# Attention without a maxima pass: exponentials taken unshifted, their sums tested, the old program kept behind a branch

## The chip, the cores and the metric

The kernel runs on one core of a Trainium2 chip. The core has five engines that matter here: TensorE (PE in the profile; its weight loads are the row PEld), VectorE (DVE), ScalarE (ACT), GpSimd (POOL) and SyncE (SP), which only issues transfers. Matmuls read SBUF and write PSUM, which has eight banks of 512 fp32 numbers on each of 128 partitions. The metric is the device time of one execution in microseconds; lower is better. The whole program is unrolled: there is no loop on the chip, so every instruction in the profile is one that was written out.

## The reference

```python
# x: [4, 512, 48, 48]; t = 48*48 = 2304 tokens, 8 heads of d = 64
hn = group_norm(x, 32 groups) * gn_scale + gn_bias
qkv = einsum('oc,bchw->bohw', qkv_w, hn) + qkv_b          # fp32, then to fp16
q, k, v = qkv.reshape(b, 3, 8, 64, t).astype(float16)
s = 64 ** -0.25                                            # as fp16
w = softmax(einsum('bhct,bhcs->bhts', q * s, k * s), axis=-1)
a = einsum('bhts,bhcs->bhct', w, v).astype(float32)
out = x + einsum('oc,bchw->bohw', proj_w, a) + proj_b
```

For each of 4 images and 8 heads there is a 2304 x 2304 matrix of scores, whose exponentials are summed along a row and multiplied by v.

## The kernel before

Channels lie on partitions: 512 channels are four chunks of 128, and chunk p of q, k and v is the head pair p. So there are 16 head pairs in all (4 images, 4 pairs), and tokens are cut into 6 blocks of 384 (TB) or 18 tiles of 128.

*Group norm* (`norm_items`, lines 138 to 176) takes statistics of x with VectorE, averages them over a group's channels with two small matmuls, and gets a factor and an offset per channel. The norm is applied later, by GpSimd, as each block of 384 tokens is needed (`load_hn`, line 185), once for k and once for q and v of every head pair.

*q, k, v of a head pair* (`pair_items`, line 179). For each block and each of q, k, v four fp32 matmuls (one for each channel chunk, line 203) accumulate in one PSUM bank; ScalarE moves the result out as fp16 (line 225). v then goes through three transposes (line 242) so that tokens lie on partitions.

*The maxima.* Softmax needs the largest score of each row before the exponentials. `max_tile` (line 250) computes the scores with the rows (queries) on partitions, 64 channels deep, and VectorE reduces each 128 x 384 tile to its maximum (line 263). `put_max` (line 265) turns minus the maximum into two fp16 numbers and moves them with small matmuls into two extra rows beside q. The product of k, with ones in those rows, and q is then the score minus its maximum.

*Attention* (`attend`, line 343). A step is one block of queries, one head, and two tiles of keys: two matmuls give scores with keys on partitions (line 358; 66 rows deep for the even head, 128 with zeros for the odd), ScalarE takes the exponential of 768 columns at once (line 366), and two steps later two matmuls multiply by v (line 373). v has a column of ones, so row 64 of the product is the sum of the exponentials. After a head's 18 key tiles, VectorE and ScalarE move the product and the sum out; every second block VectorE inverts four rows of sums, GpSimd spreads them over partitions and multiplies (lines 387 to 398).

*Projection* (`proj_items`, line 310): GpSimd widens the attention output to fp32, sixteen fp32 matmuls for each block (line 322), VectorE adds the bias and x (line 331), and SP's queue stores the result.

*The order.* While a pair is attended, the next pair's q, k, v and maxima, the previous image's projection and the next image's norm stand in a list of items with weights (0.64 for an fp32 matmul, 0.35 for two maxima). After each step as many items follow as keep their done weight in proportion to the steps. A scheduler then turns this into one queue for each engine; it keeps dependences and may move an instruction that is ready ahead of one that was written before it. Each engine works through its own queue in order.

PSUM: two double banks for scores, one for the product with v, two for maxima, one (`ps_w`) that q, k, v, transposes, moved maxima and projection share.

## Time and profile before

| what | value |
|---|---|
| runs | 4481.62, 4498.35, 4500.76 us; median 4498.35 |
| span of the profiled execution, first to last instruction | 4493.3 us |
| mean granted TensorE clock | 0.805 |
| PE busy, weight loads | 91%, 36% |
| DVE, ACT, POOL busy | 50%, 40%, 17% |

The profiled execution has no device time of its own beside its span; the median of the runs is 5 us above the span and the lowest 12 us below it. A matmul's end is modelled in the profile (a stream of them is pipelined, and the shown durations overlap), so spacing from start to start, or the chain of waits, tells what one costs. The granted clock is the share of full speed that the chip allowed TensorE; 0.50 is half speed.

### The profile page before, as it was taken

The page shows a single profiled execution, that of the slowest core. Times are in us where ns is not written, and L with a number is a line of the kernel's source. Part 1 is how long each engine was busy: PE and PEld are TensorE (multiplying, and loading weights), DVE is VectorE, ACT ScalarE, POOL GpSimd, SP SyncE. Part 2 cuts the span into 40 slices and gives each one's busy share as a digit, 9 for nine tenths or more (in the row PEclk, how much of TensorE's full clock was granted, in tenths as well). Part 3 has the DMA queues.
Part 4 walks back from the last instruction along what each step waited for, and adds up shares of the span by engine and source line. Part 5 has one row for each costly group of instructions (what it writes and reads, how often), then busy time and mean ns, then how long its engine had stood idle before and what let it go on. Part 6 is the DMA issues. An engine that isn't in the chain of part 4 may idle for free.

```text
span 4493.3 us, 39314 instructions
## 1 busy us (share of the span) xinstructions
PE 4079.8 (91%) x14320; PEld 1600.4 (36%) x14320; DVE 2251.2 (50%) x4323; ACT 1805.2 (40%) x2593; POOL 767.3 (17%) x1176
## 2 busy tenths in 40 slices
PE   5789999989999999999999999999999999999998
PEld 2233333333333433333333334333333444333344
DVE  5555455463545455465454555545355444554531
ACT  1144443435443343443434433354433433334462
POOL 3021211112121121211202112121211212112001
PEclk8687877878788987777878988787777988778789
DMA  3000000000000010000000001000000000000001
GB/s 122 0 1 1 1 1 0 1 1 1 1 1 16 20 50 0 1 1 1 1 1 8 15 15 50 0 1 1 1 1 0 8 20 16 0 1 1 1 2 41
DMA packets 21314, 44.48 MB, mean 10 GB/s; under 512 B 2688, under 2 KB 14976, under 8 KB 21120
## 3 DMA queue, kind: packets, MB, share of 16 engines
q1 hardware_dynamic: 18432, 37.76, 2.3%
q10 hardware_dynamic: 2688, 4.21, 0.3%
q8 instruction: 113, 1.85, 0.2%
q14 instruction: 81, 0.66, 0.1%
HBM read 23.08 MB, written 18.87 MB: 9 GB/s over the span
## 4 chain that ended last, share of the span: by engine, by line
PE 76%; DVE 16%; issue 3%; ACT 2%; POOL 1%; DMA 1%; POOLq 0%; SPq 0%; ACTq 0%; DVEq 0%
PE av L373 18%; PE pm L256 17%; PE ps L358 15%; DVE mx L263 13%; PE q L203 7%; PE v L203 6%; PE pr L322 6%; PE k L203 5%; PE mt L276 2%; DVE avs L387 1%; ACT p L366 1%; PE vtr L242 1%; DVE inv L392 1%; ACT sums L388 1%; POOL att L398 0%
## 5 line engine op out<-in xcount | busy, mean ns | idle before, releaser
L263 DVE TENSOR_REDUCE mx<-pm 128x1 f32<-128x384 f32 x3456 | 1844.9, 555 | 1386.1 <-PE pm L256 1271.0
L366 ACT ACTIVATE p<-ps 128x768 f16<-128x768 f32 x1728 | 1358.8, 808 | 939.1 <-PE ps L358 806.7
L373 PE MATMUL av<-p,vv 128*65 128x384 f16 x3456 | 1111.0, 398 | 18.0 <-ACT sums L388 17.9
L256 PE MATMUL pm<-ke,qe 64*128 64x384 f16 x1728 | 679.1, 393 | 109.3 <-DVE mx L263 82.5
L256 PE MATMUL pm<-ko,qo 64*128 64x384 f16 x1728 | 684.4, 396 | 66.2 <-DVE mx L263 22.4
L358 PE MATMUL ps<-qe,ke 66*128 66x384 f16 x1728 | 530.9, 362 | 7.6 <-ACT p L366 7.6
L373 PEld LDWEIGHTS <-vv 128*65 128x65 f16 x3456 | 390.5, 127 | 402.6 <-issue 278.5
L358 PE MATMUL ps<-qo,ko 128*128 128x384 f16 x1728 | 526.5, 358 | 1.6 <-ACT p L366 1.5
L388 ACT COPY sums<-av 1x384 f32<-1x384 f32 x192 | 90.3, 470 | 922.1 <-DVE avs L387 919.8
L256 PEld LDWEIGHTS <-qo 64*128 64x128 f16 x1728 | 165.9, 96 | 674.0 <-issue 673.3
L256 PEld LDWEIGHTS <-qe 64*128 64x128 f16 x1728 | 165.3, 96 | 638.6 <-issue 601.2
L387 DVE COPY avs<-av 64x384 f32<-64x384 f32 x192 | 105.0, 547 | 437.0 <-PE av L373 423.1
L322 PE MATMUL pr<-a,wproj 128*128 128x384 f32 x768 | 277.8, 504 | 19.5 <-DVE x L331 17.5
L358 PEld LDWEIGHTS <-ke 66*128 66x128 f16 x1728 | 167.7, 106 | 186.1 <-issue 135.6
L396 POOL PARTITION_BROADCAST ib<-inv x96 | 59.5, 677 | 955.9 <-DVE inv L392 754.4
L331 DVE SCALAR_TENSOR_TENSOR x<-pr,bproj,x 128x384 f32<-128x384 f32 x96 | 58.8, 612 | 325.8 <-PE pr L322 325.8
L358 PEld LDWEIGHTS <-ko 128*128 128x128 f16 x1728 | 155.9, 104 | 184.6 <-issue 138.3
L276 PE MATMUL mt<-ident,hl 128*2 128x128 f16 x576 | 89.7, 290 | 115.1 <-DVE hl L272 112.3
L322 PEld LDWEIGHTS pr<-a,wproj 128*128 128x128 f32 x768 | 142.2, 194 | 127.0 <-DVE x L331 39.6
L225 ACT ACTIVATE qe<-q,bqk 64x384 f16<-64x384 f32 x96 | 55.2, 575 | 266.1 <-PE q L203 266.0
L398 POOL TENSOR_TENSOR att<-avs,ib 128x384 f16<-128x384 f32 x96 | 93.4, 985 | 363.5 <-issue 363.5
L392 DVE RECIPROCAL inv<-sums 97x384 f32<-97x384 f32 x48 | 122.5, 2551 | 44.4 <-ACT sums L388 44.4
(815 smaller groups left out, 2508.1 us busy)
## 6 DMA issues: line engine op xcount, KB each, us to landing
x<-x_dram SPq DMA_DIRECT2D x32, 576.0 KB, 6.8
out_dram<-x SPq DMA_DIRECT2D x96, 192.0 KB, 1.9
wqkv<-qkv_wT_dram ACTq DMA_DIRECT2D x3, 1024.0 KB, 15.2
wproj<-proj_wT_dram ACTq DMA_DIRECT2D x1, 1024.0 KB, 14.0
gsc<-gn_scale_dram ACTq DMA_DIRECT2D x1, 2.0 KB, 4.0
gbi<-gn_bias_dram ACTq DMA_DIRECT2D x1, 2.0 KB, 5.6
bqkv<-qkv_b_dram ACTq DMA_DIRECT2D x1, 6.0 KB, 6.6
bproj<-proj_b_dram ACTq DMA_DIRECT2D x1, 2.0 KB, 6.3
```

What stands on the lines that cost most here:

```text
L203: nc.tensor.matmul(pw[name], wqkv[:, c, o : o + P], hn[key][:, c, :], start=(c == 0), stop=(c == NC - 1),)
L256: nc.tensor.matmul(pm, q[lo : lo + D, t0 : t0 + P], k[lo : lo + D, bass.ts(s, TB)], start=True, stop=True,)
L263: nc.vector.tensor_reduce(mx[:, h, i, s : s + 1], pm, AX.X, ALU.max)
L276: nc.tensor.matmul(pt[lo : lo + 2, bass.ts(i, P)], hl[:, h, i, :], ident, start=True, stop=True,)
L322: nc.tensor.matmul(pw[o], wproj[:, c, bass.ts(o, P)], at[0][:, c, :], start=(c == 0), stop=(c == NC - 1),)
L358: nc.tensor.matmul(ps[:, i, :TB], kk[0:rows, bass.ts(2 * s + i, P)], qq[0:rows, bass.ts(j, TB)], start=True, stop=True,)
L366: nc.scalar.activation(pt[k], ps[:, :, :TB], AF.Exp)
L373: nc.tensor.matmul(av[0], vv[:, 2 * s + i, h, :], pt[k][:, i, :], start=(s == 0 and i == 0), stop=(s == NT // 2 - 1 and i == 1),)
L387: nc.vector.tensor_copy(avs[j][h * D : (h + 1) * D, :], av[0][0:D, :])
L388: nc.scalar.copy(sm[r : r + 1, :], av[0][D : D + 1, :])
L392: nc.vector.reciprocal(inv[0:97, :], sm[0:97, :])
L398: nc.gpsimd.tensor_tensor(att[:, bass.ts(jj, TB)], avs[jj], ib, ALU.mult)
```

## The change

The old program becomes `general_path` (with block sizes renamed; nothing else in it is changed). A new `fast_path` runs first, and a branch on the chip runs the old program after it, over the same output, if any sum of exponentials lies outside 256 to 60000. In `fast_path`:

- there is no maxima pass: the exponential is taken of the score itself;
- a unit of attention is one block of 512 queries (the last has 256), both heads and one tile of keys (two in the last block): the two heads' scores are matmuls 64 rows deep on the upper and lower rows, and one exponential takes 1024 columns;
- the sums go by transfer to one number per partition, are inverted there, and come back through DRAM spread over 64 partitions; they are kept for the test;
- the norm is applied once, in place, by VectorE; x is loaded again for the sum at the end;
- v is computed with tokens on partitions (the normalised x is the stationary operand), so it isn't transposed;
- the projection's weights are split into a rounded part and the rest, both float32r, and each fp32 matmul becomes two of float32r;
- q, k and v are moved out of PSUM by VectorE; `ps_w` has two banks, and the product with v has one for each head;
- units go in bursts of two: two units' scores, then the values of the burst before, then items.

```diff
+SUM_MIN, SUM_MAX = 256.0, 60000.0
...
+    ps_s = ctx.enter_context(tc.tile_pool(name="ps_s", bufs=2, space=PSUM))
+    ps_av = ctx.enter_context(tc.tile_pool(name="ps_av", bufs=1, space=PSUM))
+    ps_w = ctx.enter_context(tc.tile_pool(name="ps_w", bufs=2, space=PSUM))
...
+    def split_wproj():
+        for c in range(NC):
+            w = work.tile([P, C], F32, tag="res", bufs=3, name=f"wproj_{c}")
+            nc.sync.dma_start(w, proj_wT[bass.ts(c, P), :])
+            nc.vector.tensor_copy(whi[:, c, :], w)
+            nc.vector.tensor_tensor(
+                wlo[:, c, :], w, whi[:, c, :].bitcast(F32), ALU.subtract
+            )
...
+    def norm(b):
...
+        for c in range(NC):
+            nc.vector.tensor_scalar(
+                hn[b][c],
+                hn[b][c],
+                ga[:, c : c + 1],
+                gb[:, c : c + 1],
+                ALU.mult,
+                ALU.add,
+            )
...
+    def qk_items(g):
...
+        def one(part, j, c, pw):
+            o, n = QBLOCKS[j]
+            if c == 0:
+                pw[0] = ps_w.tile([P, QB], F32, tag="pw", name=f"pqk_{g}_{part}_{j}")
+            w0 = part * C + pr * P
+            nc.tensor.matmul(
+                pw[0][:, :n],
+                wqkv[:, c, w0 : w0 + P],
+                hn[b][c][:, o : o + n],
+                start=(c == 0),
+                stop=(c == NC - 1),
+            )
+            if c == NC - 1:
+                col = part * NPAIR + pr
+                nc.vector.tensor_scalar(
+                    qk[g][part][:, o : o + n],
+                    pw[0][:, :n],
+                    SCALE,
+                    bqk[:, col : col + 1],
+                    ALU.mult,
+                    ALU.add,
+                )
...
+    def v_items(b):
...
+        def one(i, c, pw):
...
+            nc.tensor.matmul(
+                pw[0],
+                hn[b][c][:, bass.ts(i, P)],
+                wqkv[:, c, 2 * C :],
+                start=(c == 0),
+                stop=(c == NC - 1),
+            )
+            if c == NC - 1:
+                for pr in range(NPAIR):
+                    cols = bass.ts(pr, P)
+                    nc.vector.tensor_tensor(
+                        vv[b * NPAIR + pr][:, i, :, 0:D],
+                        pw[0][:, cols].rearrange("p (h d) -> p h d", d=D),
+                        bv[:, cols].rearrange("p (h d) -> p h d", d=D),
+                        ALU.add,
+                    )
...
+    def proj_items(b, j):
...
+            if c == 0:
+                pw[0] = ps_w.tile([P, QB], F32, tag="pw", name=f"pr_{b}_{j}_{m}")
+                pw[1] = work.tile([P, QB], F32, tag="res", bufs=3, name=f"x_{b}_{j}_{m}")
+                nc.sync.dma_start(pw[1][:, :n], x[b, bass.ts(m, P), o : o + n])
+            for i, w in enumerate((whi, wlo)):
+                nc.tensor.matmul(
+                    pw[0][:, :n],
+                    w[:, c, bass.ts(m, P)],
+                    at[0][:, c, :n],
+                    start=(c == 0 and i == 0),
+                    stop=(c == NC - 1 and i == 1),
+                )
...
+    def scores(u):
...
+        for a, i in enumerate(keys):
+            for h in range(2):
+                rows = slice(h * D, (h + 1) * D)
+                nc.tensor.matmul(
+                    ps[:, h, a * n : (a + 1) * n],
+                    k[rows, bass.ts(i, P)],
+                    q[rows, o : o + n],
+                    start=True,
+                    stop=True,
+                )
+        pt = ppool.tile([P, 2, QB], F16, tag="p", name=f"p_{g}_{j}_{keys[0]}")
+        nc.scalar.activation(pt, ps, AF.Exp)
...
+    def values(u):
...
+        for h in range(2):
+            for a, i in enumerate(keys):
+                nc.tensor.matmul(
+                    av[h][:, :n],
+                    vv[g][:, i, h, :],
+                    pt[:, h, a * n : (a + 1) * n],
+                    start=(i == 0),
+                    stop=(i == NT - 1),
+                )
...
+    def finish(g, j):
...
+        for h in range(2):
+            nc.vector.tensor_copy(avx[0 : D + 1, h, :n], av[h][:, :n])
+        first = 2 * o // P
+        sm = sums[:, g, first : first + 2 * per].rearrange("p (h i) -> p h i", h=2)
+        for h in range(2):
+            nc.sync.dma_start(sm[:, h, :], avx[D : D + 1, h, :n])
+        inv = small.tile([P, 2, QB // P], F32, tag="inv", name=f"inv_{g}_{j}")
+        nc.vector.reciprocal(inv[:, :, :per], sm)
+        row = dram.tile([2, QB], F32, tag="row", name=f"row_{g}_{j}")
+        nc.sync.dma_start(
+            row[:, :n].rearrange("h (p i) -> p h i", i=per), inv[:, :, :per]
+        )
+        ib = work.tile([D, 2, QB], F32, tag="ib", name=f"ib_{g}_{j}")
+        nc.sync.dma_start(
+            ib[:, :, :n], row[:, :n].unsqueeze(0).to_broadcast((D, 2, n))
+        )
+        for h in range(2):
+            nc.vector.tensor_tensor(
+                atts[g][h * D : (h + 1) * D, o : o + n],
+                avx[0:D, h, :n],
+                ib[:, h, :n],
+                ALU.mult,
+            )
...
+    beside = {g: [] for g in range(NG)}
+    for b in range(B):
+        g = b * NPAIR
+        for pr in (2, 3):
+            beside[g + pr - 2] += qk_items(g + pr)
+        if b > 0:
+            for j in range(NQ):
+                late = b == B - 1
+                beside[g + (2 + j // 3 if late else j // 4)] += proj_items(b - 1, j)
+        if b + 1 < B:
+
+            def turn(b=b):
+                hn[b + 1] = load_x(b + 1, (nc.gpsimd, nc.gpsimd))
+                norm(b + 1)
+
+            beside[g + 2].insert(0, (0.0, turn))
+            vs = v_items(b + 1)
+            beside[g + 2] += [(45.0, lambda: None)] + vs[:55]
+            beside[g + 3] += vs[55:]
+            for pr in (0, 1):
+                beside[g + 3] += qk_items(g + NPAIR + pr)
+
+    norm(0)
+    for _, run in qk_items(0):
+        run()
+    split_wproj()
+    for _, run in v_items(0) + qk_items(1):
+        run()
...
+    for n in range(0, len(stream), 2):
+        burst = stream[n : n + 2]
...
+            scores(u)
+        for u in waiting:
+            values(u)
+        waiting = burst
+        fill(n + len(burst) - 1)
...
+    nc.vector.tensor_scalar(low, flat, SUM_MIN, None, ALU.is_ge)
...
+    nc.vector.scalar_tensor_tensor(both, flat, SUM_MAX, low, ALU.is_le, ALU.mult)
...
+    nc.vector.tensor_reduce(good, both, AX.X, ALU.add)
...
+    nc.tensor.matmul(pf, good, ones, start=True, stop=True)
+    nc.vector.tensor_scalar(flag, pf, float(B * HEADS * T) - 0.5, None, ALU.is_lt)
...
+    fast_path(tc, flag, *args)
+    fails = nc.values_load(
...
+    with tc.If(fails > 0):
+        general_path(tc, *args)
```

A number beside an item is its weight; `fill` runs a pair's items in proportion to the units done, as the old list did. The weight of 45 runs nothing: it only holds back what follows it.

More of the change, by code (lines that the diff above doesn't have):

```diff
@@ L12 @@
 F32 = mybir.dt.float32
+F32R = mybir.dt.float32r
 F16 = mybir.dt.float16
+I32 = mybir.dt.int32
 AF = mybir.ActivationFunctionType
@@ L25, with general_path @@
 NPAIR = HEADS // 2
-TB = 384
-NB = T // TB
+NG = B * NPAIR
 NT = T // P
-TPB = TB // P
 SCALE = float(np.float16(1.0 / math.sqrt(math.sqrt(D))))
 LAG = 2
+GTB = 384
+GNB = T // GTB
+GTPB = GTB // P
+QB = 512
+QBLOCKS = [(o, min(QB, T - o)) for o in range(0, T, QB)]
+NQ = len(QBLOCKS)
+SB = 384
+SUM_MIN, SUM_MAX = 256.0, 60000.0
 @with_exitstack
-def group_norm_attention(
+def general_path(
     ctx: ExitStack,
@@ L347, in attend @@
         atts[g] = att
-        steps = [(j, h, s) for j in range(NB) for h in range(2) for s in range(NT // 2)]
+        steps = [(j, h, s) for j in range(GNB) for h in range(2) for s in range(NT // 2)]
         total = sum(w for w, _ in items) or 1.0
@@ L390, in values @@
                 return
-            inv = work.tile([P, TB], F32, tag="inv", name=f"inv_{g}_{j}")
+            inv = work.tile([P, GTB], F32, tag="inv", name=f"inv_{g}_{j}")
             nc.vector.reciprocal(inv[0:97, :], sm[0:97, :])
@@ L398, in values @@
                 nc.gpsimd.tensor_tensor(
-                    att[:, bass.ts(jj, TB)], avs[jj], ib, ALU.mult
+                    att[:, bass.ts(jj, GTB)], avs[jj], ib, ALU.mult
                 )
@@ L450, with group_norm_attention @@
+@with_exitstack
+def group_norm_attention(ctx: ExitStack, tc: tile.TileContext, *args):
+    nc = tc.nc
+    keep = ctx.enter_context(tc.tile_pool(name="keep", bufs=1))
+    flag = keep.tile([1, 1], I32, name="flag")
+    fast_path(tc, flag, *args)
+    fails = nc.values_load(
+        flag[0:1, 0:1],
+        min_val=0,
+        max_val=1,
+        skip_runtime_bounds_check_because="it is the result of a comparison",
+    )
+    with tc.If(fails > 0):
+        general_path(tc, *args)
 def kernel(
```

295 lines of the change are left out of this document (259 added, 36 removed).

## The prediction

> **What bounds the kernel now.** I read the busy times first, then the chain of waits, then the costliest groups.
>
> ```profile
> span 4493.3 us, 39314 instructions
> PE 4079.8 (91%) x14320; PEld 1600.4 (36%) x14320; DVE 2251.2 (50%) x4323; ACT 1805.2 (40%) x2593; POOL 767.3 (17%) x1176
> ...
> PE 76%; DVE 16%; issue 3%; ACT 2%; POOL 1%; DMA 1%; POOLq 0%; SPq 0%; ACTq 0%; DVEq 0%
> PE av L373 18%; PE pm L256 17%; PE ps L358 15%; DVE mx L263 13%; PE q L203 7%; PE v L203 6%; PE pr L322 6%; PE k L203 5%; PE mt L276 2%; DVE avs L387 1%; ACT p L366 1%; PE vtr L242 1%; DVE inv L392 1%; ACT sums L388 1%; POOL att L398 0%
> ...
> L263 DVE TENSOR_REDUCE mx<-pm 128x1 f32<-128x384 f32 x3456 | 1844.9, 555 | 1386.1 <-PE pm L256 1271.0
> L366 ACT ACTIVATE p<-ps 128x768 f16<-128x768 f32 x1728 | 1358.8, 808 | 939.1 <-PE ps L358 806.7
> ```
>
> The chain is PE three quarters of the time, and the maxima pass alone (the matmuls into pm, the reductions into mx, the move into mt) holds 17 + 13 + 2 = 32% of it, some 1440 us. ACT and DVE have slack. But the pass costs more than its 32%. The view of busy time by stretches, with the granted clock in the column after POOL, shows it:
>
> ```profile
> 200.00:4300.00 4100.00, 3780.95 (x13293) 1467.38 (x13292) 2103.86 (x4032) 1684.62 (x2417) 689.69 (x1061) 0.80 0.02 6
> 4320.00:4410.00 90.00, 86.49 (x443) 48.12 (x442) 13.04 (x17) 82.76 (x116) 13.64 (x20) 0.97 0.02 5
> 4425.00:4490.00 65.00, 51.76 (x146) 25.87 (x145) 11.17 (x19) 0.00 (x0) 7.68 (x17) 1.00 0.15 55
> ...
> 1928.00:1932.00 4.00, 2.86 (x7) 0.51 (x5) 3.94 (x8) 0.00 (x0) 0.00 (x0) 0.50 0.00 0
> ```
>
> From 200 to 4300 us, where maxima run, the clock is 0.80. In the last pair, which has attention and no maxima left, it is 0.97 while ACT is busy 82.76 of 90 us; in the closing projection it is 1.00 although PE waits a fifth of the time for evictions. The low clock sits where PE waits for DVE's maxima (the 4 us row: DVE 3.94 busy, seven matmuls, clock 0.50). So the pass goes, and the clock should come back with it.
>
> **What one matmul costs at full clock.** From the chain in order of time, and from the order on PE:
>
> ```profile
> 1502.69 2.58 PE pr L322 x8
> 1508.83 0.33 PE av L373 x2
> 1509.16 0.33 PE ps L358 x2
> ```
>
> ```profile
> 1945.96 0.33 PE L256 MATMUL pm<-ke,qe 64*128 64x384 f16 x1
> 1945.97 0.33 PE L256 MATMUL pm<-ko,qo 64*128 64x384 f16 x1
> 1946.23 0.52 PE L373 MATMUL av<-p,vv 128*65 128x384 f16 x2
> ...
> 1946.91 0.33 PE L373 MATMUL av<-p,vv 128*65 128x384 f16 x1
> 1947.16 0.33 PE L256 MATMUL pm<-ke,qe 64*128 64x384 f16 x1
> ```
>
> An fp32 matmul is two instructions (768 of pr for 384 matmuls), each 2.58/8 = 0.3225 us at 384 columns, so 0.43 at 512 and 0.215 at 256. An fp16 matmul of 384 takes 0.33/2 = 0.165, half as long as an fp32 instruction; at 512 I take half of 0.43, 0.215. The second fence holds the two prices on which the packed scores rest. Two matmuls of 64 rows, one on each half of the rows, start 0.01 apart and the next matmul starts 0.26 later: the pair runs at once. And that 0.26, like the 0.25 from av into pm, is 0.10 more than 0.165: changing between 64-row and 128-row matmuls costs 0.10 each way.
>
> **The change, part by part.**
>
> *Removed:* the 3456 matmuls and reductions of the maxima, mt and vtr, and ACT's evictions of q, k, v.
>
> *Attention.* 16 head pairs x (4 blocks x 18 + 9) = 1296 units. Each has one packed pair of scores (0.215), two products with v (0.43), and half of the two row changes of a burst of two units (0.10): 0.745 us, 966 in all. Weight loads I take as hidden, as in the chain above where each matmul has its own; if those of one pair can't load under the pair before, up to 0.10 more per unit by the row change, +130. Below 0.745 it can't go, since the row changes are in the order.
>
> *q, k:* per pair 2 x 4 channel chunks x (4 x 0.86 + 0.43) = 31.0, times 16 = 495. *v:* the same columns with tokens as the stationary side, 288 x 0.86 = 248, without transposes. *Projection:* each fp32 matmul becomes two of float32r. No row shows that type. Bounds: as costly as an fp16 pass (0.215 for 512), 4 x 16 x 2 x (4 x 0.215 + 0.108) = 124; or as an fp32 matmul each, four times that, 495. I take 124, since the instruction reads one rounded operand, which is nearest to the fp16 row. The Trainium skill ("FP8 and Floating Point Precision", TensorE Precision Notes) gives true FP32 four passes and describes a reduced FP32 read; the 0.3225 against 0.165 agrees with two passes in each of two instructions, and no run here shows the reduced form.
>
> PE's sum at full clock: 966 + 495 + 248 + 124 = 1833.
>
> *ACT* has nothing left but exponentials of 1024.
>
> ```profile
> 4359.78 4.43 ACT L366 ACTIVATE p<-ps 128x768 f16<-128x768 f32 x6
> ...
> L225 ACT ACTIVATE ke<-k,bqk 64x384 f16<-64x384 f32 x96 | 55.2, 575 | 161.3 <-PE k L203 161.0
> ```
>
> Back to back one of 768 takes 0.738. Scaled wholly it is 0.985 for 1024; with the slope between 575 and 808 ns (0.61 ns a column) 0.89. I take 0.94: 1218 in all (1153 to 1277), below PE. A unit of attention alone is 0.745 on PE against 0.94 on ACT, so wherever the fillers are missing ACT sets the pace: the first half of each third pair (a weight of 45 stands there for the loading of the next image, against 47 of v: 39 units x 0.195 = 8, three times) and the last pair (60 + 10 of PE work against 76). Together +30.
>
> *DVE* takes q, k, v evictions, the norm's application and the divisions. By the 612 ns of a 384 eviction, 160 of q and k and 80 of the projection at 0.82 are 196, 288 small ones of v about 0.35 are 100, and four of 512 for each of 80 blocks another 260: about 650 with the norm, a third of the span. It hides, unless it waits.
>
> *Waits added.* At each of the 80 block ends DVE copies, then waits for the sums to come back over SP's queue, inverts, waits for a write and a broadcast read, and multiplies. Rows for such transfers:
>
> ```profile
> out_dram<-x SPq DMA_DIRECT2D x96, 192.0 KB, 1.9
> ...
> gsc<-gn_scale_dram ACTq DMA_DIRECT2D x1, 2.0 KB, 4.0
> ```
>
> Three in series are 5.7 to 12 us. Behind the waiting reciprocal stand the evictions of q, k, v, and behind those PE, which has a second ps_w bank: one more group of four matmuls (3.4 us) and the attention among it (about 3) before it stops. So 0 to about 6 us each, 0 to 480. The order on DVE isn't the text's order, which speaks for little:
>
> ```profile
> 27.38 0.56 DVE L145 BATCH_NORM_STATS2 st<-x 128x6 f32<-128x384 f32 x1 [5.10 <-DMA x<-x_dram]
> 27.86 0.14 DVE L152 COPY mean<-gmean 128x4 f32<-128x4 f32 x1
> 27.92 0.55 DVE L145 BATCH_NORM_STATS2 st<-x 128x6 f32<-128x384 f32 x1
> ```
>
> The second image's statistics, written far behind, run between steps of the first image's norm. Work that is ready is put between waiting steps, so I take 0.75 us each, 60, with the norm's two matmuls and a late image in it. The Trainium skill ("DMA: Bandwidth & Descriptors") puts a fixed cost of about 2.0 us on every transfer. By it the chain is 6 us, at the low end, and the 60 would be nearer to nothing; the 4.0 of gsc says that small ones take longer.
>
> *Other queues.* SP takes four transfers a block (320) and, in the projection, a load of x and a store for each of 80 groups, in order: an x behind a row that waits for the reciprocal is late by the same chain, which is within the 6 us. The bytes are no matter: the closing row above has a DMA share of 0.15 at 55 GB/s. POOL has casts in place of the norm. The next image is loaded into the one set of x buffers only when its predecessor's q and k are done; the weight of 45 gives that 39 x 0.94 = 37 us, against some 40 for the load and norm at the start (next fence). Where it is late, PE has attention left to do, and each us beyond that is lost, three times.
>
> *Start.*
>
> ```profile
> 22.43 0.56 PE L150 MATMUL gmean<-mv,gmat 128*128 128x4 f32 x2 [22.43 <-DVE mv L146]
> ...
> 35.12 4.23 PE L203 MATMUL k<-hn_('k', 0)_203,wqkv 128*128 128x384 f32 x8 [5.22 <-POOL hn_('k', 0)_203 L189]
> ```
>
> Now k needs whole chunks normalised by DVE, 4 x 2304 columns, at 0.55/384 a column 13 us or less, in place of POOL's first block, and the second image's statistics aren't in between (about 5 less): 34 to 43, taken as 40.
>
> *End.* The last block's division, its projection, the test of the sums, the flag's load into the engines and a branch past the old program: 20 that nothing covers (10 to 40; the first block's transfers above are its largest part).
>
> *Clock.* 0.975, between the 0.97 and 1.00 of the stretches without maxima: 2.5% of about 1950, 49.
>
> Sum: 1833 + 30 + 60 + 40 + 20 + 49 = 2032 as a span. The median of the runs shown is 5 us over the profiled span, so 2037; I say **2040**, with its own range 1920 to 2160. The fall from 4498 is the pass and its clock.
>
> **The rivals.**
>
> *The clock stays low.* For it: 0.50 also held from 1960 to 1964 in the row below with PE wholly busy, and the change makes many 64-row matmuls; attention at ACT's pace leaves PE 20% idle. Against it: 0.97 and 1.00 in the stretches above, with PE as idle. At 0.805: (1833 + 60)/0.805 + 90 = 2440. Decides if the clock column in mid-kernel stays below 0.85. 10%. The Trainium skill ("TensorE: Matmul & The Clock Gate", A second HAM failure mode) has a kernel cycling through PSUM whose clock oscillates between half and full; that is this rival.
>
> ```profile
> 1960.00:1964.00 4.00, 4.00 (x11) 0.89 (x11) 2.05 (x4) 0.96 (x2) 0.00 (x0) 0.50 0.00 0
> ```
>
> *The pairs don't overlap* or their loads lie open, so that the packing doesn't do what it says: +130 with open loads, +279 (1296 x 0.215) one after another: 2170 to 2320. The 0.01 above speaks against it. 9%.
>
> *float32r costs two or four passes:* +124 or +371, 2165 to 2410. 8%.
>
> *Block ends stop PE,* 6 us for each of 80 rather than 0.75: +420, 2460. Shown by a long idle time of PE before a group of k, q or v. 9%.
>
> *Slower than before: the branch is taken.* If one of 73,728 sums lies outside 256 to 60000, or reads so, the whole old program runs after the new one: 2040 + 4493 = 6530. From the reference's inputs I work out sums between 2747 and 6732 and a largest exponential of 486, well inside, so only a fault in the sums' way would do it. 2%.
>
> **How the numbers follow.** 62% for the forecast; the rivals hold 38%. 1920 to 2420 takes in the forecast and the packing and float32r rivals, and leaves out the low clock, the block ends, the branch and a little below: about 2 in 10. Half a per cent, 22 us, is what a measurement here can tell from no change; all cases but the branch are far below it: faster 0.97, same 0.01, slower 0.02.
>
> **What would show it.** Right: no pm or mx; PE over 85% of the chain; granted clock 0.95 or more; the exponential 0.9 to 1.0 us; scores of both halves starting together; a float32r matmul of 512 spaced 0.215. Wrong: a clock near 0.8, DVE or DMA over a tenth of the chain, a span above 2200, or groups of the old program in it.

## The result, and the profile after

The changed kernel takes **2034.48 us** (median of four runs, 2030.16 to 2035.5). The kernel before, on the same chip, takes 4494.34 (4481.62 to 4500.76). The ratio is 0.4525, with a 95% interval of 0.4517 to 0.4534. The forecast was 2040, in a range of 1920 to 2420.

The page of the kernel after: the span, the busy times, the granted clock in 40 slices, and its costliest groups (busy time and mean of one, then the idle time in front of them and what ended it).

```profile
span 2032.8 us, 21633 instructions
...
PE 1948.3 (96%) x8274; PEld 852.8 (42%) x8274; DVE 520.3 (26%) x1101; ACT 1243.3 (61%) x1297; POOL 66.1 (3%) x134
...
PEclk9999999899999999899999999989999999999999
...
L763 ACT ACTIVATE p<-ps 128x1024 f16<-128x1024 f32 x1296 | 1242.0, 1038 | 719.9 <-PE ps L755 668.7
L777 PE MATMUL av<-p,v 128*65 128x512 f16 (+1 forms) x2880 | 730.7, 368 | 25.9 <-DVE avx L792 25.9
L624 PE MATMUL pqk<-x,wqkv 128*128 128x512 f32 (+1 forms) x1280 | 556.1, 552 | 4.1 <-DVE x L598 4.1
L755 PE MATMUL ps<-q,k 64*128 64x512 f16 (+1 forms) x2880 | 435.5, 362 | 8.4 <-ACT p L763 6.0
```

No group of the maxima and none of the old program is in it. TensorE is busy 96% of the span, its idle column is nearly empty, and the clock stands at 9 in 37 of 40 slices and at 8 in the others (0.989 over the span, against 0.805). ScalarE's 719.9 us of idle time are nearly all spent waiting for scores (141 of them ahead of the first exponential), as a second engine behind the bound should. The chain that the page follows back breaks off after some 7% of the span, so the bound is read from the busy times and from the order on TensorE.

The view by stretches (length, busy time of PE, PEld, DVE, ACT and POOL, then clock, DMA share and GB/s) shows four kinds of stage: the start without exponentials, a part of the middle, the attention of the last pairs, and the closing projection.

```profile
33.00:155.00 122.00, 122.00 (x292) 56.04 (x292) 32.45 (x93) 0.00 (x0) 0.00 (x0) 1.00 0.00 0
...
1450.00:1750.00 300.00, 298.44 (x1285) 125.92 (x1284) 62.49 (x123) 207.76 (x216) 0.61 (x1) 1.00 0.05 11
1770.00:1800.00 30.00, 27.59 (x113) 19.95 (x112) 10.40 (x14) 0.00 (x0) 6.87 (x12) 1.00 0.73 230
1830.00:1970.00 140.00, 138.53 (x661) 47.92 (x660) 25.68 (x49) 138.77 (x152) 0.00 (x0) 1.00 0.10 22
1985.00:2026.00 41.00, 33.70 (x146) 24.31 (x144) 14.86 (x24) 0.00 (x0) 8.30 (x16) 0.97 0.67 210
```

In the middle TensorE is full and ScalarE is busy 208 of 300 us. In the last pairs ScalarE is full (138.77 of 140). The third row is one that the prediction had no word for: 30 us in which ScalarE does nothing at all, in the middle of the attention. The experiment with the earlier projection takes it up.

The order on TensorE in mid-kernel (start, time from there to the end of the last of the group, group):

```profile
599.59 1.88 PE L624 MATMUL pqk<-x,wqkv 128*128 128x512 f32 x4
601.40 0.61 PE L755 MATMUL ps<-q,k 64*128 64x512 f16 x6
601.93 1.05 PE L777 MATMUL av<-p,v 128*65 128x512 f16 x4
602.82 2.74 PE L624 MATMUL pqk<-x,wqkv 128*128 128x512 f32 x6
605.50 0.61 PE L755 MATMUL ps<-q,k 64*128 64x256 f16 x8
```

Two units' scores, values and fillers follow each other as written. The group of scores at 601.40 takes 0.53 us until the values start: two pairs at 0.22 and a row change of 0.09. By the single starts in the trace, the two matmuls of a pair begin 3 to 4 ns apart, and the next pair begins 0.226 us after the first of them. A pair before values takes 0.310 (0.084 more), a matmul of values before scores 0.314 (0.098 more than 0.216), and an fp32 instruction before scores 0.525 (0.096 more than 0.429). So the packing works, and its price is close to what was read from before: 0.226 a pair where 0.215 was taken, and 0.08 to 0.10 a change.

### The profile page after: what moved, and what is told of

Its sections match the earlier page's. It is cut to its first block, busy times and chain, and to the rows that moved or that the text cites. A ratio compares the mean times of both kernels' runs of the same rounds, so it can differ in the third digit from the quotient of the medians.

```text
span 2032.8 us, 21633 instructions
## 1 busy us (share of the span) xinstructions
PE 1948.3 (96%) x8274; PEld 852.8 (42%) x8274; DVE 520.3 (26%) x1101; ACT 1243.3 (61%) x1297; POOL 66.1 (3%) x134
## 5 line engine op out<-in xcount | busy, mean ns | idle before, releaser
L763 ACT ACTIVATE p<-ps 128x1024 f16<-128x1024 f32 x1296 | 1242.0, 1038 | 719.9 <-PE ps L755 668.7
L777 PE MATMUL av<-p,v 128*65 128x512 f16 (+1 forms) x2880 | 730.7, 368 | 25.9 <-DVE avx L792 25.9
L624 PE MATMUL pqk<-x,wqkv 128*128 128x512 f32 (+1 forms) x1280 | 556.1, 552 | 4.1 <-DVE x L598 4.1
L755 PE MATMUL ps<-q,k 64*128 64x512 f16 (+1 forms) x2880 | 435.5, 362 | 8.4 <-ACT p L763 6.0
L777 PEld LDWEIGHTS <-v 128*65 128x65 f16 x2880 | 262.9, 111 | 387.4 <-issue 294.6
L755 PEld LDWEIGHTS <-k 64*128 64x128 f16 x2880 | 125.3, 94 | 453.5 <-issue 448.9
L624 PEld LDWEIGHTS pqk<-x,wqkv 128*128 128x128 f32 x1280 | 241.6, 191 | 151.1 <-issue 98.9
L670 PE MATMUL pv<-wqkv,x 128*128 128x512 f32 x576 | 263.7, 593 | 0.0
L714 PE MATMUL pr<-a,whi 128*128 128x512 f32 (+1 forms) x320 | 131.5, 416 | 11.8 <-POOL a L704 7.1
L714 PE MATMUL pr<-a,wlo 128*128 128x512 f32 (+1 forms) x320 | 120.1, 380 | 0.0
## 6 DMA issues: line engine op xcount, KB each, us to landing
wqkv<-qkv_wT_dram ACTq DMA_DIRECT2D x3, 1024.0 KB, 10.9
```

The costliest lines, as they stand in the source:

```text
L624: nc.tensor.matmul(pw[0][:, :n], wqkv[:, c, w0 : w0 + P], hn[b][c][:, o : o + n], start=(c == 0), stop=(c == NC - 1),)
L670: nc.tensor.matmul(pw[0], hn[b][c][:, bass.ts(i, P)], wqkv[:, c, 2 * C :], start=(c == 0), stop=(c == NC - 1),)
L714: nc.tensor.matmul(pw[0][:, :n], w[:, c, bass.ts(m, P)], at[0][:, c, :n], start=(c == 0 and i == 0), stop=(c == NC - 1 and i == 1),)
L755: nc.tensor.matmul(ps[:, h, a * n : (a + 1) * n], k[rows, bass.ts(i, P)], q[rows, o : o + n], start=True, stop=True,)
L763: nc.scalar.activation(pt, ps, AF.Exp)
L777: nc.tensor.matmul(av[h][:, :n], vv[g][:, i, h, :], pt[:, h, a * n : (a + 1) * n], start=(i == 0), stop=(i == NT - 1),)
```

## The experiments

Each kernel was compared with the kernel before on the same chip; a time without an interval is that of a single run. The first four take the change apart, the next five test the costs it adds, and the last three follow what was found on the way.

### The maxima: the wait on VectorE, or the matmuls

The kernel before, with only the first 64 of a tile's 384 columns reduced:

```diff
-                nc.vector.tensor_reduce(mx[:, h, i, s : s + 1], pm, AX.X, ALU.max)
+                nc.vector.tensor_reduce(
+                    mx[:, h, i, s : s + 1], pm[:, 0:64], AX.X, ALU.max
+                )
```

> The kernel before, with VectorE reducing 64 of each 384 scores instead of all (the shift is then the maximum of a sixth of the keys; everything else is computed). TensorE does all its work of the maxima pass, VectorE about 1100 us less. Theory A (the clock falls because TensorE waits for VectorE's maxima): the granted clock rises from 0.80 to 0.95 or more, and the time falls to TensorE's own work at that clock, 2950 to 3250 us. Theory B (the clock falls because of the mixture of 64-row and 128-row matmuls itself): the clock stays between 0.78 and 0.85 and the time stays above 3500 us.

Measured: 3384.38 us, beside 4498.09 for the kernel before. The page's group of the reductions, and the stretch from 200 to 3300 us:

```profile
L263 DVE TENSOR_REDUCE mx<-pm 128x1 f32<-128x64 f32 x3456 | 644.2, 219 | 1499.7 <-PE pm L256 1496.5
```

```profile
200.00:3300.00 3100.00, 3026.84 (x13711) 1327.61 (x13709) 979.49 (x4018) 1761.70 (x2538) 700.47 (x1077) 0.98 0.02 9
```

TensorE does the same matmuls in the same mixture, and its clock is 0.98 where it was 0.80. What changed is that it is busy 98% of the stretch and not 92%: its short waits for VectorE are nearly gone. That settles the main step of the prediction, that the clock comes back with the pass, and it puts the cause on the waits on the reductions, not on the mixture of 64-row and 128-row matmuls alone. The rows of the kernel before show the order of events just ahead of the stretch from 1960 to 1964, which the prediction's rival quotes for a clock of 0.50 with TensorE wholly busy:

```profile
1952.00:1956.00 4.00, 2.87 (x10) 0.79 (x10) 4.00 (x9) 0.00 (x0) 0.00 (x0) 1.00 0.00 0
1956.00:1960.00 4.00, 3.36 (x10) 0.82 (x10) 2.16 (x5) 1.94 (x3) 0.00 (x0) 0.53 0.02 4
```

TensorE waits behind a VectorE that is busy all the time, and then the clock falls. The clock records of that trace change in steps of 3.41 us. Counted in such steps, all 52 in which TensorE stood idle for 30% or more at full clock ended with a fall to half, against 19 of the 621 in which it was idle for under 5%. Those 19, and 9 falls in this run that come with TensorE busy throughout, aren't explained by waits; whether the mixture has a share in them stays open.

The time is above theory A's range. TensorE is busy 3218 of the 3382 us, so the excess is its own work: from start to start, waits included, the matmuls of ps, av and pm take 0.217, 0.214 and 0.190 us in the mean, where the prediction's rows have 0.165 for one without a change of rows.

The Trainium skill ("TensorE: Matmul & The Clock Gate", HAM oscillation — how this bites in real kernels) ties a low clock to idle gaps of TensorE of more than some 3.4 us, in a kernel that waits for transfers. The direction agrees, the size doesn't: from 200 to 4300 us of the kernel before TensorE's longest wait is 1.9 us, and the clock is 0.80. The Trainium skill ("TensorE: Matmul & The Clock Gate", A second HAM failure mode), whose case is a rival in the prediction, has a kernel that cycles through PSUM banks, idles briefly between groups of matmuls, and sees its clock oscillate between half and full. Brief waits and such a clock are what the kernel before shows. The kernel after cycles through its banks too, has few such waits and stands at 0.989, so the cycling by itself doesn't lower the clock here.

Next, the kernel before without any maxima (the two extra rows of q are zero):

```diff
+        nc.gpsimd.memset(qe[D : D + 2, :], 0.0)
...
-            for i in range(TPB):
-                for s in range(NB):
-                    items.append(
-                        (0.35, lambda j=j, i=i, s=s, mx=mx: max_tile(j, i, s, mx[0]))
-                    )
-            items.append((0.3, lambda j=j, mx=mx: put_max(j, mx[0])))
```

> The kernel before without its maxima pass and nothing else changed (no maxima, no moved shift; the two extra rows of q are zero, so the exponential is unshifted). Theory A (the pass and its clock carry most of the change): TensorE's remaining work is 2131 us at full clock; with a clock of 0.97 and some waiting for the one bank that q, k, v and the projection share, 2250 to 2400 us, leaving 220 to 370 us to the packing, the cheaper projection and the new order. Rival (the packing and the new order carry as much as the pass): above 2700 us.

Measured: 2454.07 us. From its page, the busy times and the chain by engine and by line:

```profile
PE 2286.7 (93%) x10288; PEld 1267.5 (52%) x10288; DVE 380.5 (16%) x579; ACT 1697.1 (69%) x2401; POOL 770.3 (31%) x1178
...
PE 68%; ACT 14%; issue 8%; POOL 5%; DVE 3%; DMA 2%; ACTq 0%; POOLq 0%; DVEq 0%
PE ps L347 15%; PE av L362 15%; PE pr L311 11%; PE v L204 10%; PE k L204 9%; PE q L204 8%; ACT p L355 8%; ACT qo L226 2%; ACT qe L226 2%; ACT vt L240 1%; POOL att L387 1%; PE vtr L243 1%; DVE inv L381 1%; ACT sums L377 1%; DVE st L146 1%
```

So of the 2464 us from 4498 to 2034, 1114 are the waits on the reductions and the clock they cost (4498 to 3384), 930 the rest of the pass (3384 to 2454), and 420 everything else in the change (2454 to 2034). The pass alone is 83% of the gain. The time is 54 above the range. TensorE is busy 2287 us, 156 more than the 2131 that the expectation counted, so most of the miss is in the size of its own work. ScalarE holds 14% of the chain: 8% are exponentials, the rest moves out of PSUM.

### The packed scores

The kernel after, with both heads' scores on the same 64 rows of TensorE; the odd head uses the even head's q and k.

```diff
-                rows = slice(h * D, (h + 1) * D)
+                rows = slice(0, D)
```

> The changed kernel with both heads' scores on the same 64 rows, so that two score matmuls can't run at once (the odd head then uses the even head's q and k: its attention is not the reference's, the work is the same). Theory A (TensorE bounds the changed kernel and a pair costs as much as one matmul): each of 1296 units costs up to 0.215 us more, less in the stretches that ScalarE paces: 2240 to 2310 us. Rival (something else bounds it, the pairing is worth little): below 2100 us.

Measured: 2336.95 us, 302 more than the kernel after. The same place on TensorE:

```profile
600.67 1.03 PE L755 MATMUL ps<-q,k 64*128 64x512 f16 x4
601.63 1.05 PE L777 MATMUL av<-p,v 128*65 128x512 f16 x4
```

Four scores now take 0.96 us until the values start, against 0.53: 0.215 more a unit, 279 for 1296 units, as the prediction's rival had it. The clock is lower as well, 0.963:

```profile
PEclk9999998899999999699999999957999999999999
```

Three slices stand at 5 to 7, in which the kernel after has 8 or 9. Span times mean clock is 2249 here and 2010 there, so by that rough account some 240 of the 302 are matmuls (279 is the bound, for less is lost where ScalarE sets the pace) and some 60 the clock. The low stretches begin where TensorE stands still, at the turns from one image to the next. The first of them:

```profile
384.90:388.30 3.40, 0.00 (x0) 0.00 (x0) 0.00 (x0) 0.76 (x1) 0.00 (x0) 1.00 0.68 270
388.30:429.30 41.00, 36.13 (x76) 8.30 (x75) 18.70 (x39) 17.30 (x17) 1.04 (x1) 0.50 0.06 10
```

The kernel after has the same stops (the part on waits below shows one), each with some 10 us of half clock behind it. Here half clock lasts 41, 38 and 82 us at the three turns, although TensorE is busy 36.13 of the first 41. Why it lasts so long isn't settled.

### The projection in two parts

The projection as one fp32 matmul, as before:

```diff
-            for i, w in enumerate((whi, wlo)):
-                nc.tensor.matmul(
-                    pw[0][:, :n],
-                    w[:, c, bass.ts(m, P)],
...
+            nc.tensor.matmul(
+                pw[0][:, :n],
+                wproj[:, c, bass.ts(m, P)],
```

> The changed kernel with the projection as one fp32 matmul in place of two of float32r. Theory A (two float32r passes cost 0.47 us for 512 columns against 0.86 for one fp32 matmul, and the projection lies on the path): 64 x (4 x 0.39 + 0.195) = 113 us more, 2120 to 2160 us. Rival (the projection is hidden beside the exponentials): 2040 to 2080 us.

Measured: 2127.3 us, 93 more, so the float32r pass is far nearer to an fp16 pass than to fp32. Its price stands in the closing projection of the kernel after (order on TensorE):

```profile
1985.08 0.39 PE L714 MATMUL pr<-a,whi 128*128 128x512 f32 x1
1985.31 0.39 PE L714 MATMUL pr<-a,wlo 128*128 128x512 f32 x1
```

0.23 us from start to start (0.231 and 0.234 are the usual values), where fp16 has 0.216 and an fp32 matmul 0.86 in its two instructions. The packing (302, some 60 of them clock) and the projection (93) are 395 of the 420. But what the parts cost when each is undone by itself need not add up to the gain: a single bank costs another 102 (below). v without transposes and VectorE's evictions were not undone.

### The end of a block

One more transfer in the chain of each block end, from DRAM to DRAM:

```diff
+        row2 = dram.tile([2, QB], F32, tag="row2", name=f"row2_{g}_{j}")
+        nc.sync.dma_start(row2[:, :n], row[:, :n])
...
-            ib[:, :, :n], row[:, :n].unsqueeze(0).to_broadcast((D, 2, n))
+            ib[:, :, :n], row2[:, :n].unsqueeze(0).to_broadcast((D, 2, n))
```

> The changed kernel with one more transfer (DRAM to DRAM) in the chain at each of 80 block ends, which makes each chain some 2 to 3.5 us longer. Theory A (the second bank and the order on VectorE hide those chains): less than 15 us more. Rival (block ends stop TensorE): 160 to 280 us more.

Measured: 2042.83 us, ratio 0.4544 (0.4535 to 0.4553), 8 more. VectorE's waits for the broadcast (total, times, longest), first after, then here:

```profile
DVE att L808 <- DMA ib<-row: 291.7, 73, 6.6
```

```profile
DVE att L810 <- DMA ib<-row: 340.3, 73, 8.9
```

VectorE waits some 49 us longer and the kernel loses 8. So the chain is covered, 0.1 us a block for one more transfer, and the rival by which every block end stops TensorE falls. What covers it this run doesn't tell; the next kernel takes away one candidate, the second bank of `ps_w`.

With one bank for `ps_w`:

```diff
-    ps_w = ctx.enter_context(tc.tile_pool(name="ps_w", bufs=2, space=PSUM))
+    ps_w = ctx.enter_context(tc.tile_pool(name="ps_w", bufs=1, space=PSUM))
```

> The changed kernel with one PSUM bank instead of two for q, k, v and the projection. Theory A (the second bank matters where no attention lies between two groups: 38 groups before the first scores and the last projection, about 1 us each, and 0.2 us at the 250 others): 60 to 110 us more. Rival (evictions are exposed at each of 312 groups): 250 us more or above.

Measured: 2136.38 us, ratio 0.4752 (0.4743 to 0.4762), 102 more. TensorE's waits here:

```profile
PE pr L714 <- DVE x L723: 38.5, 37, 3.6
...
PE av L777 <- DVE avx L792: 16.9, 9, 9.5
PE pqk L624 <- DVE k L633: 6.7, 7, 2.1
PE pqk L624 <- DVE x L723: 6.4, 2, 4.5
```

In the kernel after the first row is 4.7 us, 4 times. TensorE now stops at groups that wait for the eviction of the one before, mostly for 0.84 us at a time. That is about one eviction (0.75 in VectorE's rows further down), not the chain of a block end. Its idle time from the first matmul of k on is 97 us against 46 in the kernel after, so 51 of the 102 are waits of TensorE; where the rest sits wasn't located. The second bank is worth 102 us, but that it is what hides the chain isn't shown.

### The bursts, the branch

Bursts of one unit:

```diff
-    for n in range(0, len(stream), 2):
-        burst = stream[n : n + 2]
+    for n in range(0, len(stream), 1):
+        burst = stream[n : n + 1]
```

> The changed kernel with bursts of one unit instead of two, so that TensorE changes between 64-row and 128-row matmuls twice as often. Theory A (each change costs 0.10 us, and TensorE bounds): up to 648 x 0.19 = 123 us more, less in the stretches that ScalarE paces: 2100 to 2160 us. Rival (the changes are hidden, or fewer exponentials in flight matter more): below 2060 or above 2200.

Measured: 2168.76 us, ratio 0.4824 (0.4814 to 0.4833), 134 more. The number of row changes doubles: 648 more bursts, each with one change of 0.084 and one of 0.098, are 118. Values that wait for their exponential, of which the kernel after has none in its view of waits, add 10.9 (46 times). So the second measurement of the price comes within some 5 us of the first, and the 130 that the prediction put into the attention for the changes is close.

Without the flag's load, the branch and the old program:

```diff
     fast_path(tc, flag, *args)
-    fails = nc.values_load(
...
-    with tc.If(fails > 0):
-        general_path(tc, *args)
```

> The changed kernel without the flag's load, the branch and the old program behind it (the sums are still tested). Theory A (the guard costs little that shows): 2025 to 2034 us. Rival (the load of the flag into all engines and the branch over the old program cost part of what the end holds): 2010 to 2020 us.

Measured: 2031.24 us, ratio 0.4518 (0.4509 to 0.4527), not told apart from 0.4525 (0.4517 to 0.4534). And with the branch taken, by a lower bound of 4000 for the sums:

```diff
-SUM_MIN, SUM_MAX = 256.0, 60000.0
+SUM_MIN, SUM_MAX = 4000.0, 60000.0
```

> The changed kernel with the test's lower limit at 4000 instead of 256, so that some sums of these inputs fall below it and the old program runs after the new one over the same output. The prediction's rival on the slower side: 2034 + 4493 = 6530 us, 6500 to 6560. If the two overlapped or the old program ran otherwise than alone, it would show as another sum.

Measured: 6515.14 us. Its two halves by stretches:

```profile
0.00:2000.00 2000.00, 1923.13 (x8176) 835.47 (x8176) 511.79 (x1087) 1243.41 (x1297) 60.30 (x122) 0.99 0.14 38
...
2060.00:6500.00 4440.00, 4065.86 (x14293) 1597.22 (x14294) 2232.26 (x4274) 1803.60 (x2592) 748.50 (x1155) 0.80 0.02 7
```

2034 and some 4480 are added, and within one execution the clock goes from 0.99 to 0.80 as the old program begins. Taken branch: 45% slower than before; not taken: too little to be measured.

### The 48 us in which ScalarE stands still

By the prediction's prices the 14th pair takes 91 us (60 of attention and 31 of q and k for the 16th); from its first exponential to that of the next it took 139.5. ScalarE's longest wait in the kernel after, and VectorE's order around its end:

```profile
ACT p L763 <- PE av L777: 49.3, 2, 48.3
```

```profile
1799.35 0.75 DVE L723 SCALAR_TENSOR_TENSOR x<-pr,bproj,x 128x512 f32<-128x512 f32 x1 [1.46 <-DMA x<-x_dram]
1801.42 3.15 DVE L808 TENSOR_TENSOR att<-avx,ib 64x512 f16<-64x512 f32 x4 [1.31 <-POOL a L704]
```

From some 1766 to 1806 TensorE does the third image's projection in one block. The first division of the 14th pair waits until 1801.42, and is released by POOL's read of the last of the attention outputs for that projection (the bracket of the last row). The attention outputs have five tiles: four held by the third image's pairs, one by the 13th, so the 14th needs one back. But the third image's projection stands beside the 15th and 16th pairs in the list (the two lines on `late`), behind the pair that waits for its end, and so the order written for the engines draws all of it ahead. The rest of the images have theirs beside the first two pairs. Theory C is that reading; its test is to put the third projection there as well:

```diff
-                late = b == B - 1
-                beside[g + (2 + j // 3 if late else j // 4)] += proj_items(b - 1, j)
+                beside[g + j // 4] += proj_items(b - 1, j)
```

> The changed kernel with the third image's projection beside pairs 12 and 13, as the other images' is, instead of 14 and 15. Theory C (pair 13 stops because the attention outputs have five tiles: its first block can be divided only when the third image's projection has freed one, so the projection is pulled forward as one block of 45 us in which ScalarE idles): no idle time of ScalarE above 12 us in mid-kernel, pair 13 takes 95 to 105 us instead of 139, pair 12 118 to 125 instead of 95, and the sum falls by 10 to 25 us to 2010 to 2025. Rival (the scheduler pulls the projection together for another reason): the block stays, 2030 to 2040 us.

Measured: 2024.17 us, ratio 0.4501 (0.4494 to 0.4509), 10 less. The 14th pair takes 99.4 us, the 13th 124.9 instead of 95, and the stretch that held the stop has ScalarE busy 70 of 90 us:

```profile
1740.00:1830.00 90.00, 87.31 (x424) 39.31 (x422) 19.75 (x35) 70.23 (x74) 1.17 (x2) 0.98 0.13 29
```

So the reading holds. The stop cost 10 us and not 48, because TensorE worked through it (27.59 of 30 us in the stretch shown above) and it is TensorE that sets the end.

### q, k, v and projection in fp16

With everything else hidden behind TensorE, the largest term left is its fp32 work. This kernel rounds the normalised x and all weights to fp16, so each fp32 matmul becomes one pass of lower precision than in the kernel after. The edit also gives the normalised x tiles of its own, drops GpSimd's casts for the projection, and lowers the weight of 45 to 12, so its gain is that of all of these together. The core of it:

```diff
-    wqkv = const.tile([P, NC, 3 * C], F32, name="wqkv")
+    wqkv = const.tile([P, NC, 3 * C], F16, name="wqkv")
...
-    whi = const.tile([P, NC, C], F32R, name="whi")
-    wlo = const.tile([P, NC, C], F32R, name="wlo")
+    wproj = const.tile([P, NC, C], F16, name="wproj")
...
+            hpool.tile([P, T], F16, tag=f"h{c}", name=f"hn_{b}_{c}")
```

> The changed kernel with q, k, v and the projection computed from fp16 operands in one pass (the normalised x and the weights are rounded to fp16; no split weights, no casts on GpSimd). Theory A (TensorE's queue bounds the changed kernel, with 943 us of it in these matmuls): they shrink to 1280/4 x 0.86 + 288 x 0.215 + 320 x 0.215, about 250 us in all, TensorE's sum falls to 1250, just above ScalarE's 1296 x 0.92 = 1192, and with start and end about 1380 us (1330 to 1460). Rival (a wait or ScalarE takes over at once): above 1550 us.

Measured: 1558.44 us (1557.01 to 1559.11), ratio 0.3467 (0.3461 to 0.3473): 476 less than the kernel after, and 98 above the upper end of what I expected. ScalarE's waits show part of it:

```profile
ACT p L756 <- PE ps L748: 161.4, 246, 17.8
ACT p L756 <- PE av L770: 59.2, 3, 43.8
```

The stop is there again, 43.8 us, and with less TensorE work to cover it. Eight tiles for the attention outputs instead of five:

```diff
-    apool = ctx.enter_context(tc.tile_pool(name="apool", bufs=5))
+    apool = ctx.enter_context(tc.tile_pool(name="apool", bufs=8))
```

> The fp16 kernel of before (q, k, v and the projection in one fp16 pass) with eight tiles for attention outputs instead of five. Theory C: the same stop costs it more, since TensorE has less to do; with eight tiles no projection holds up a pair, the block near 1300 us goes, and the time falls from 1558 by 45 to 110 us, to 1450 to 1515. Rival (TensorE and ScalarE are each 80 to 90% busy and lose by alternating): less than 20 us.

Measured: 1525.88 us (1523.13 to 1528.07), ratio 0.3395 (0.339 to 0.3401), 33 less. Its waits of ScalarE and its busy times:

```profile
ACT p L756 <- PE ps L748: 168.7, 272, 18.2
...
ACT p L756 <- PE av L770: 1.3, 1, 1.3
```

```profile
PE 1380.2 (91%) x7026; PEld 530.4 (35%) x7026; DVE 516.8 (34%) x1097; ACT 1243.0 (82%) x1297; POOL 36.2 (2%) x66
```

The stop is gone and the gain lies between the two expectations: the tiles were a cause, but not of all of the miss. TensorE at 91% and ScalarE at 82% are now close to each other, so neither is covered by the other all the time; where the rest of the miss sits was not taken further. This is the fastest kernel of the study, faster than both.

## Why the prediction was right

**What bounds.** Right: the pass went and the clock came back with it (0.97 and 1.00 in the quiet stretches of before, 0.989 after). That the clock hung on the waits for VectorE was argued from one row of 4 us; the narrow reduction and the count of falls bear it out for most of the falls.

**The sum.** The total was met to 6 us, but partly by luck: errors of 64, 14, 7, 13 and 29 us cancel. Between its first matmul of k and its last matmul, 32.66 to 2025.72, TensorE needs 1993 us: 1947 from start to start, which are 1927 at full clock and 20 for a clock of 0.990 there, and 46 of idle time. Both ends:

```profile
32.66 17.57 PE L624 MATMUL pqk<-x,wqkv 128*128 128x512 f32 x38 [4.11 <-DVE x L598]
...
2025.92 0.15 DVE L898 TENSOR_SCALAR flag<-count 1x1 int32<-1x1 f32 x1 [1.57 <-PE count L897]
```

| term | predicted | measured |
|---|---|---|
| TensorE's work, with the stretches that ScalarE paces | 1833 + 30 | 1927 |
| waits of TensorE | 60 | 46 |
| start | 40 | 33 |
| end | 20 | 7 |
| clock | 49 | 20 |
| sum | 2032 | 2033 |

- *TensorE's work* was under-sized by 64, 3.4%. Each matmul charged with the time until the next one starts, without idle time, attention takes 1002 us (966 predicted), q and k 527 (495), v 257 (248) and the projection 159 (124), the low clock included. In these a change of rows after a filler is charged to the filler: 317 after q or k, 90 after v and 57 after the projection, 0.096 each, or 30, 9 and 5 us. That is nearly all of the overrun of q, k and v, so attention's own overrun is some 80. The other terms that I can name are the float32r pass of 0.231 to 0.234 in place of 0.215 (about 10) and the score pairs at 0.226 in place of 0.215 (1296 times 0.011, 14). Much of the rest is in spacings above their own median: values to values of 512 columns take 0.230 in the mean against 0.216 in the median, 21 us over 1543 of them. How much of that is the low clock, how much the pace of ScalarE, which the 30 stood for, isn't told apart.
- *Waits* were put at 60, 0.75 for each of the 80 block ends with the norm and a late image in it; all idle time of TensorE is 46, and it sits elsewhere. 25.9 are the values that wait for the copy (line 792, in the groups above). Of these, 9.5, 4.5 and 5.8 us are three single stops at 363, 852 and 1339 us, at the turns to the next image; the other block ends cost next to nothing. A further 11.8 lie in front of projection matmuls, most of them in the closing projection, and 8.4 in front of scores. The first of the three turns:

```profile
350.00:355.00 5.00, 3.42 (x24) 1.90 (x24) 4.56 (x12) 5.00 (x6) 0.72 (x2) 1.00 1.02 401
355.00:358.00 3.00, 0.00 (x0) 0.00 (x0) 0.30 (x1) 0.15 (x1) 0.00 (x0) 1.00 0.95 374
358.00:368.00 10.00, 4.70 (x14) 1.25 (x13) 6.54 (x16) 1.94 (x2) 0.00 (x0) 0.51 0.11 31
```

  The load of the next x fills the DMA engines (share 1.02 and 0.95). The write of the inverted sums, issued at 350.67, is followed by the broadcast read only at 358.04, and VectorE's division and copy stand behind that. So "the bytes are no matter" was wrong at this turn, where the chain met the load. The clock drops there too: about 17 of the 20 us in the row on the clock belong to the three turns. The reason given for the small price of the others, that ready work is put between waiting steps, fits the +8 of the longer chain; the part of the second bank in it isn't shown.
  The chain itself was sized between 5.7 and 12 us. Its three transfers, by the view of transfers of the kernel after (KB each, median us from issue to landing), take 2.0, 2.3 and 3.5, so 7.8; the 4.0 of gsc was not typical of small ones:

```profile
ib<-row SPq DMA_DIRECT2D x64, 256.0 KB, 3.5
...
sums<-avx SPq DMA_DIRECT2D x128, 2.0 KB, 2.0
...
row<-inv SPq DMA_DIRECT2D x64, 4.0 KB, 2.3
```

- *Start and end* were each too long by 7 and 13. The closing projection hides more of the end than I allowed, and its waits count in the idle time above; the last matmul is followed only by the flag, one more addition of x and its store.
- *Clock:* 0.975 was the middle of two stretches, 0.97 and 1.00; the 0.990 lies nearer the upper one.

**ScalarE.** The exponential of 1024 was put at 0.94 us between two ends; back to back it takes 0.904 to 0.920, while the mean of one in the groups is 1038 ns with its overlap. The Trainium skill ("ScalarE: Activation LUTs", What ACT_TABLE_LOAD costs) gives 186 ns plus 0.833 ns an element less 93 ns of overlap: an estimate of 946 ns, 3 to 5% above the trace. The last pair took 75.9 us from its first exponential to the end of its last, 76 predicted: there ScalarE sets the pace, as said.

**The rivals.** *The clock stays low* falls with 0.989. *Pairs don't overlap* falls with the 3 to 4 ns; undone, the packing costs 302, some 240 in matmuls, where up to 279 were worked out, and some 60 in clock. *float32r in two or four passes* falls: 0.231 to 0.234. *Block ends stop TensorE* falls with +8 for a longer chain; only the three turns have something of it. *The branch is taken* is what it would have cost, 6515 against 6530, and it isn't taken.

**What was missed.** The three turns, and the stop at the 14th pair. For the latter, the prediction followed queues and banks, and not the number of tiles that hold attention outputs until a projection listed far behind frees them. That stop cost 10 us, below what it takes to spoil the sum.

## What to carry to other kernels

A pass on a second engine that TensorE waits for in short gaps costs twice, once in the gaps and once in the clock: look at the granted clock of the stretch before pricing the pass by its share of the chain (here 32% of the chain, and 83% of a gain of 2464 us). When everything is moved behind one engine, the sum of its spacings from start to start forecasts the time; check then each pool of buffers for a tile that is freed by work listed behind the work that needs it, and each chain of small transfers for a large load beside it. Once TensorE has less to do, such a stop costs more: the same five tiles cost 10 us with fp32 work to cover them and 33 without.

## What the runs showed of the hardware that I had not expected

- A float32r matmul of 512 columns is spaced 0.231 to 0.234 us, 8% more than the fp16 one at 0.216. The nearest row had suggested none.
- A change between 64-row and 128-row matmuls costs 0.08 to 0.10 us each way, nearly the same in both kernels and by the bursts of one (+134 for 648 more bursts, some 11 of them waits for exponentials). The Trainium skill ("TensorEngine Tiling (Array Packing)", Key Properties) says that a change of tiling mode drains TensorE, without a figure; the trace agrees and gives one.
- In the kernel before, waits of at most 1.9 us were enough to bring the clock to half, when they took 30% or more of a step of 3.41 us. In the kernel with unpacked scores three stops of TensorE brought half clock for 41, 38 and 82 us, in the kernel after for some 10 each. No run here tells why it lasted longer.
